# A second level of seven products inside four of the block products of q, k and v

## The chip, the cores and the metric

The kernel runs on one core of a Trainium2 chip. The metric is device time in microseconds (us) of one execution. TensorE (PE) multiplies, VectorE (DVE), ScalarE (ACT) and GpSimd (POOL) do elementwise work, SyncE (SP) issues most of the DMA transfers. A matmul reads a stationary operand of 128 x 128, loaded by its own instruction (PEld), and streams the columns of the other operand past it. Results go to PSUM, in tiles that are handed from engine to engine by semaphores.

## The reference

Two graph layers over 4096 nodes with 512 features, each followed by a residual sum and a layer norm. The first is a masked additive attention with 4 heads. The second, cut to what matters here, is

```
q = einsum('nd,hdk->hnk', x, Wqs)      # x: 4096 x 512, 8 heads of 64
k = einsum('nd,hdk->hnk', x, Wks)
v = einsum('nd,hdk->hnk', x, Wvs)
scores = einsum('hqk,hmk->hqm', q, k) / 8 + 0.01 * eye - 1e16 * (1 - adj)
x = layernorm(x + einsum('hqm,hmk,hko->qo', softmax(scores), v, Wo))
```

So q, k and v are each a product of a 4096 x 512 matrix and a 512 x 512 matrix, all in fp32.

## The kernel before

The program has three stages on its time line: layer 0 (to about 1126 us), the q, k, v stage (to about 1420 us), and the attention of layer 1 (to the end). All engines work through queues in the written order.

**The q, k, v stage.** The loop `for pair in range(NG // 2)` goes over four pairs of 512 rows, and calls `gemm` three times in each: k, q, v. In a gemm the 1024 rows by 512 features of a pair and the 512 x 512 weights are each cut into 2 x 2 blocks (`features(pair, c, n)`, `block(w, m, c)`), and the block product is done with seven products instead of eight. The products have numbers, and `order = (1, 5, 2, 6, 7, 3, 4)` is the order in which TensorE does them. Products 5, 6, 7 and 3 read sums of weight blocks (`combine_weights`, tables `of_weights`, `wk_s`, `wq_s`, `wv_s`), and products 5, 6, 7 and 4 read sums of feature blocks (`combine_features`, `x_s`). The sums of the weights are made once, in the gemms of pair 0; those of the features are made for each pair, in the v gemm of the pair before, on VectorE (L1176).

A product is 2 x 2 x 2 chunk products of 128 features by 128 outputs by 256 rows. For k and q (L1208) it is four matmuls of 512 columns; for v (L1201), in which the features are the stationary operand, eight of 256 columns. An fp32 matmul is two passes on TensorE, each with its own weight load, and the profile counts passes. Products 2, 3 and 4 accumulate onto the PSUM tile of products 1, 5 and 7.

The results leave PSUM thus: ScalarE copies product 1 to `u2`, product 5 to `p5`, and product 1 + 2 to the first output block (L1215); VectorE adds product 6 onto `u2` and `u2` onto the others (L1236); GpSimd adds `p5` to the fourth block (L1230). `store` sends blocks to DRAM from SP's queue. PSUM holds three tiles of two banks (`s_ps`) and two tiles of one bank (`x_ps`).

What a gemm does beside its products is in a table `beside`: after product i the functions of `beside[i]` are issued. Here lie the loads of the next rows (`bring`), their transposes on VectorE (`turn`, L975), the sums of weights and features, and, in the last pair, the loads for the attention (`load_adjT`, `load_q`, `load_kv`). `Later` holds steps that are issued some products later; in the first two gemms these are the layer norms that end layer 0 (`normal_factors`, four small GpSimd instructions each, L514 to L519).

In SBUF the tag `adjT1` has 11 places, for blocks of the mask in the attention. In the q, k, v stage `spare()` lends them to the sums.

**Attention.** In the last v gemm, before product 4, TensorE does the scores of the first three units (`score`, L1138), so that the attention's pipeline is full when the gemm ends. In the attention TensorE alternates between scores (L1138) and products with v (L1424).

Of the kernel before, what the change touches and what calls it, by code (L numbers as in the profile page):

```python
# [429 lines left out]
def tile_gat_then_masked_attention(  # L430
# [666 lines left out]
    with wait_by_tile("l1", 1) as l1, wait_by_tile("l1a", 2) as lp, \  # L1097
# [46 lines left out]
        with wait_by_tile("l1s", 2) as sp:  # L1144
# [9 lines left out]
            def spare():  # L1154
# [4 lines left out]
            wq_s = {5: wq_s[0][:, 0], 6: wq_s[0][:, 1], 3: wq_s[1][:, 0], 7: block(wq, 1, 0)}  # L1159
            wv_s = {i: sp.tile([P, 2, D // 2], F32, name=f"wv_s{i}", bufs=1) for i in (5, 6, 3)}  # L1160
            wv_s[7] = block(wv, 1, 0)
            x_s = {i: spare().rearrange("p a b r -> p (a b r)").rearrange(
                "p (c r) -> p c r", c=2) for i in of_features}

            def features(pair, c, n):
                return xTs[2 * pair + n][:, 2 * c:2 * c + 2, :]

# [5 lines left out]
            def combine_features(engine, pair, i):  # L1173
                a, c, op = of_features[i]
                a, c = (x_s[k] if isinstance(k, int) else features(pair, *k) for k in (a, c))
                engine.tensor_tensor(x_s[i], a, c, op=op)  # L1176
# [4 lines left out]
            def gemm(w, sums, kind, pair, beside):  # L1181
# [5 lines left out]
                u2, p5 = (sp.tile([P, 2 * G], F32, name=n, bufs=2) for n in ("u2", "p5"))  # L1187
# [4 lines left out]
                def product(i, t, more=False):  # L1192
                    a = block(w, *plain_weights[i]) if i in plain_weights else sums[i]
                    x = features(pair, *plain_features[i]) if i in plain_features else x_s[i]
                    for n in range(2):
                        half = t[0][:, n * G:(n + 1) * G] if len(t) == 1 else t[n]
                        if kind == "v":
                            half = half.rearrange("p (t d) -> p t d", t=2)
                            for r in range(2):
                                for c in range(2):  # L1200
                                    nc.tensor.matmul(  # L1201
                                        half[:, r, :],
                                        x[:, c, (2 * n + r) * P:(2 * n + r + 1) * P], a[:, c, :],
                                        start=not more and r == 0 and c == 0, stop=c == 1,
                                        skip_group_check=True)
                        else:
                            for c in range(2):
                                nc.tensor.matmul(half, a[:, c, n * P:(n + 1) * P], x[:, c, :],  # L1208
                                                 start=not more and c == 0, stop=c == 1,
                                                 skip_group_check=True)  # L1210

# [20 lines left out]
                def add(dst, t):  # L1232
                    n = 2 * G // len(t)
                    for k, src in enumerate(t):
                        part = slice(k * n, (k + 1) * n)
                        nc.vector.tensor_tensor(dst[:, part], src, u2[:, part], op=ALU.add)  # L1236

                t = {}
                for i in order:
                    if i == (7 if last else 1 if kind == "k" and pair == 0 else 0):  # L1240
                        t[i] = [xp.tile([P, GT, P], F32, name="x_ps").rearrange(
                            "p t r -> p (t r)") for _ in range(2)]
                    elif i in (1, 5, 6, 7):
                        t[i] = new()
                    else:
                        t[i] = t[{2: 1, 3: 5, 4: 7}[i]]
                    if i == 4 and last:
                        for n in range(3):
                            first[n] = score(0, 0, n)
                            nc.scalar.activation(first[n], first[n], AF.Exp, scale=float(KD) ** -0.5)  # L1250
# [8 lines left out]
                    elif i == 6:  # L1259
                        add(u2, t[i])  # L1260
                    elif i == 7:
                        add(out["22"], t[i])
                        pool(out["22"], out["22"], p5, ALU.add)
                        later.at(1, lambda: store("22"))
                    elif i == 3:
                        add(out["12"], t[i])
                        store("12")
                    elif last:
                        copy(out["21"], t[i])
                        pool(out["21"], out["21"], u2, ALU.add)  # L1270
                        store("21", nc.gpsimd)
                    else:
                        add(out["21"], t[i])
                        store("21")
                    for fn in beside.get(i, []):
                        fn()
                    later.step()

            for pair in range(NG // 2):
# [10 lines left out]
                beside = {}  # L1290
                if pair == 0:
                    combine_features(nc.vector, 0, 5)
                    for n, i in ((1, 6), (5, 7), (2, 3)):
                        beside.setdefault(n, []).append(
                            lambda i=i: combine_weights(nc.vector, wk, wk_s, i))
                    for n, i in ((1, 6), (5, 7), (2, 4)):
                        beside.setdefault(n, []).append(
                            lambda i=i: combine_features(nc.vector, 0, i))
                    for i, n in ((5, 7), (6, 7), (7, 3), (3, 4)):
                        beside.setdefault(n, []).append(  # L1300
                            lambda i=i: combine_weights(nc.gpsimd, wq, wq_s, i))
                if more:
                    for k, n in ((5, 0), (7, 1)):
                        beside.setdefault(k, []).append(lambda n=n: bring(n))
                if pair == 0:
                    beside.setdefault(4, []).append(lambda: load_all(wv, wvs))
                gemm(wk, wk_s, "k", pair, beside)
                beside = {}
                if pair == 0:
                    for i, n in ((5, 5), (6, 2), (7, 6), (3, 7)):  # L1310
                        beside.setdefault(n, []).append(
                            lambda i=i: combine_weights(nc.gpsimd, wv, wv_s, i))
                if more:
                    for k, fn, n in ((1, turn, 0), (5, turn, 1), (5, bring, 2), (6, bring, 3),
                                     (4, turn, 2)):
                        beside.setdefault(k, []).append(lambda fn=fn, n=n: fn(n))
                else:
                    for c in range(3):
                        load_adjT(0, c)
                    load_q(0, 0)  # L1320
                gemm(wq, wq_s, "q", pair, beside)
                beside = {}
                if more:
                    beside[1] = [lambda: turn(3)]
                    for i, n in ((5, 5), (6, 6), (7, 7), (4, 4)):
                        beside.setdefault(n, []).append(
                            lambda i=i: combine_features(nc.vector, pair + 1, i))
                else:
                    beside[5] = [lambda: load_kv(0, 0, 0)]
                    beside[2] = [lambda: [load_adjT(0, c) for c in range(3, NCJ - 2)],  # L1330
                                 lambda: [finish_md(0, t) for t in range(GT)]]
                    beside[7] = [lambda: load_kv(0, 0, 1),
                                 lambda: [load_adjT(0, c) for c in range(NCJ - 2, NCJ)]]
                gemm(wv, wv_s, "v", pair, beside)
# [282 lines left out]
```

## Time and profile before

| | |
|---|---|
| median of three runs | 3333.77 us (3333.41 to 3334.64) |
| profiled execution, its own time | 3333.58 us |
| its span, first to last instruction | 3331.7 us |
| granted TensorE clock | 0.998 |
| PE busy | 3310.5 us, 99% |
| DVE, ACT, POOL busy | 72%, 59%, 63% |
| k or q gemm | 24.0 us |
| v gemm | 24.17 us |

The page gives the busy time of each engine, the chain of work that ended last, and groups of instructions by line. In a row of the timeline, the first number is the start in us from the span's start, the second the duration of the instruction or of the group (`x8` is eight instructions), then engine, line, operation, output and inputs; in brackets stands the idle time before it and what ended it. Names lose their numbers, and a lent tile bears the name of its place: `adjT` in this stage is a sum of weights or features, and `p` is often `p5`. A row of the table of stretches has the stretch, its length, busy time and instructions of PE, PEld, DVE, ACT and POOL, the granted clock, the busy share of the DMA engines and GB/s.

### The profile page before, as it was taken

Reading aid. Unit: us, or ns where it says so; the run is one execution under the profiler, and the core shown is the slowest. Engines: PE = TensorE matmul, PEld = TensorE weight load, DVE = VectorE, ACT = ScalarE, POOL = GpSimd, SP = SyncE. Lnnn points to the kernel's source line nnn. Section 1 sums busy time; section 2 is a strip of 40 time slices with the busy share of each in tenths; the row PEclk is TensorE's granted clock in tenths of the full one; section 3 lists DMA queues with packets and bytes.
Section 4 is the critical chain, followed back from the end, with each engine's and each line's share of the span. In section 5 each row is a group of like instructions: output and inputs, shape, how many; then the busy total and the mean of one; then the engine's idle time right before and its main releaser. Section 6 shows DMA issues by size and latency. Waiting matters only on the chain.

```text
span 3331.7 us, 66521 instructions
## 1 busy us (share of the span) xinstructions
PE 3310.5 (99%) x26968; PEld 1938.6 (58%) x26968; DVE 2403.4 (72%) x3005; ACT 1955.9 (59%) x2419; POOL 2106.7 (63%) x1535
## 2 busy tenths in 40 slices
PE   9999999999999999999999999999999999999998
PEld 8899999999999756633333333333333333333333
DVE  6789899898999633266767666666766766667666
ACT  1367968878766311156656556566565656656654
POOL 5630040040030310189999999999999999999996
PEclk9999999999999999999999999999999999999999
DMA  8989786686532443489898988989888799887984
GB/s 180 229 203 184 220 185 169 152 181 146 137 93 58 115 147 111 160 198 212 191 214 224 225 204 189 211 191 253 206 191 210 188 208 251 193 211 185 211 198 112
DMA packets 398989, 612.01 MB, mean 184 GB/s; under 512 B 167632, under 2 KB 248528, under 8 KB 398672
## 3 DMA queue, kind: packets, MB, share of 16 engines
q0 software_dynamic: 97520, 258.77, 42.6%
q1 hardware_dynamic: 299280, 345.88, 33.3%
q8 instruction: 214, 3.51, 0.4%
q10 hardware_dynamic: 1872, 3.02, 0.4%
q14 instruction: 103, 0.84, 0.1%
HBM read 315.87 MB, written 109.25 MB: 128 GB/s over the span
## 4 chain that ended last, share of the span: by engine, by line
PE 95%; POOL 2%; DMA 1%; DVE 1%; issue 1%; ACT 0%; SPq 0%; POOLq 0%; DVEq 0%
PE o_ps L1087 27%; PE o_ps L1424 26%; PE s_ps L1138 25%; PE s_ps L1208 6%; PE o_ps L846 4%; PE s_ps L1488 3%; PE s_ps L1201 3%; DMA p<-p 1%; PE s_ps L1443 1%; POOL q_sum L1399 0%; DMA y_sb<-in_x_dram 0%; DVE p L1556 0%; POOL s L699 0%; PE x_ps L1201 0%; PE x_ps L1208 0%
## 5 line engine op out<-in xcount | busy, mean ns | idle before, releaser
L1399 POOL TENSOR_TENSOR q_sum<-q_sum,p 128x1024 f32<-128x1024 f32 x538 | 1373.0, 2552 | 63.8 <-DMA p<-p 38.1
L1379 DVE TENSOR_TENSOR p<-s_ps,adjT 128x1024 f32<-128x1024 f32 x896 | 1044.0, 1216 | 464.8 <-ACT s_ps L1376 437.3
L1376 ACT ACTIVATE s_ps<-s_ps 128x1024 f32<-128x1024 f32 x1021 | 967.3, 1006 | 594.4 <-PE s_ps L1138 591.6
L1138 PE MATMUL s_ps<-q_sb,k_sb 64*64 64x512 f32 x8192 | 943.0, 589 | 0.7 <-DVE p L1379 0.7
L1424 PE MATMUL o_ps<-p,v_sb 64*64 64x512 f32 x8192 | 943.6, 590 | 0.0
L1087 PE MATMUL o_ps<-sup_t,p 128*128 128x129 f32 x8192 | 915.7, 275 | 1.2 <-DVE p L640 1.2
L1087 PEld LDWEIGHTS o_ps<-sup_t,p 128*128 128x128 f32 x8192 | 915.3, 192 | 1.7 <-DVE p L640 1.4
L640 DVE SCALAR_TENSOR_TENSOR p<-fr_t,dj,az 128x1024 f32<-128x1024 f32 x512 | 650.4, 1284 | 67.1 <-PE o_ps L1087 38.9
L1138 PEld LDWEIGHTS s_ps<-q_sb,k_sb 64*64 64x64 f32 x8192 | 312.7, 133 | 567.0 <-issue 455.4
L1424 PEld LDWEIGHTS o_ps<-p,v_sb 64*64 64x64 f32 x8192 | 310.3, 133 | 570.6 <-issue 561.2
L624 ACT ACTIVATE z<-fr_t,f 128x1024 fp8e4<-128x1024 f32 x512 | 557.2, 1143 | 101.6 <-DVE az L635 101.5
L1409 POOL DMA_DIRECT2D p<-p x412 | 437.7, 1300 | 9.3 <-PE o_ps L1424 8.4
L1063 POOL DMA_DIRECT2D agg<-base_d x32 | 29.0, 1215 | 386.8 <-DMA sup_t<-sup_d 204.7
L585 POOL COPY seen<-token 128x1 f32<-128x1 f32 x24 | 11.4, 476 | 356.4 <-DVE token L583 356.4
L1379 DVE TENSOR_TENSOR p<-s_ps,md 128x1024 f32<-128x1024 f32 x128 | 150.6, 1217 | 69.4 <-ACT s_ps L1376 64.4
L635 DVE TENSOR_TENSOR az<-adjT,z 128x512 int32<-128x512 int32 x256 | 175.3, 685 | 1.9 <-ACT z L624 0.7
L1230 POOL TENSOR_TENSOR k_sb<-k_sb,p 128x1024 f32<-128x1024 f32 x12 | 30.7, 2560 | 192.1 <-DVE k_sb L1236 187.8
L600 ACT ACTIVATE adjT<-stage 128x1024 fp8e4<-128x1024 bf16 x128 | 130.8, 1050 | 17.8 <-DMA stage<-adj_d 17.8
L1215 ACT ACTIVATE u<-s_ps 128x1024 f32<-128x1024 f32 x11 | 11.3, 1024 | 173.4 <-PE s_ps L1208 110.1
L1488 PE MATMUL s_ps<-wo_sb,on 128*128 128x512 f32 x240 | 110.8, 604 | 0.0
L1458 ACT ACTIVATE r<-r_h 32x256 f32<-32x256 f32 x248 | 102.3, 412 | 2.9
L1236 DVE TENSOR_TENSOR u<-s_ps,u 128x1024 f32<-128x1024 f32 x12 | 14.7, 1225 | 106.2 <-PE s_ps L1208 76.3
(194 smaller groups left out, 2094.4 us busy)
## 6 DMA issues: line engine op xcount, KB each, us to landing
p<-p POOLq DMA_DIRECT2D x412, 512.0 KB, 9.1
k_sb<-k_d SPq DMA_DIRECT2D x128, 512.0 KB
v_sb<-v_d SPq DMA_DIRECT2D x128, 512.0 KB
adj_d<-in_adj_dram POOLq DMA_DIRECT2D x32, 1024.0 KB, 11.3
sup_t<-sup_d SPq DMA_DIRECT2D x120, 258.0 KB
fr_t<-fr_d SPq DMA_DIRECT2D x16, 1024.0 KB
adjT_d<-adjT SPq DMA_DIRECT2D x32, 512.0 KB
adjT<-adjT_d SPq DMA_DIRECT2D x32, 512.0 KB
```

What stands on the lines that cost most here:

```text
L624: nc.scalar.activation(z[:, k, :], fr_t[w, h][:, 0, :], AF.Sign, bias=fs[j // GT][:, 0, (j + k) % GT, h:h + 1], saturate=False)
L635: nc.vector.tensor_tensor(az.bitcast(I32), adjT[w, j // CJ][:, j % CJ:j % CJ + 2, :].bitcast(I32), z.bitcast(I32), op=ALU.bitwise_and)
L640: nc.vector.scalar_tensor_tensor(p, fr[:, 1, :], dj[j // GT][:, j % GT, h:h + 1], az_t[w, h, j // 2][:, j % 2, :], op0=ALU.max, op1=ALU.mult)
L1087: nc.tensor.matmul(o[t // BK][:, t % BK, :], p[:, t * P:(t + 1) * P], s, start=(j == 0 and t % BK == 0), stop=(j == NT - 1), skip_group_ch ...
L1138: nc.tensor.matmul(s[c:c + MS, e, :], k[r, a + c:a + c + MS], qt[g, m][r, :], start=True, stop=True)
L1208: nc.tensor.matmul(half, a[:, c, n * P:(n + 1) * P], x[:, c, :], start=not more and c == 0, stop=c == 1, skip_group_check=True)
L1376: nc.scalar.activation(s, s, AF.Exp, scale=float(KD) ** -0.5)
L1379: nc.vector.tensor_tensor(p, s, keep[:, None, :].to_broadcast([P, HP, G]), op=ALU.mult)
L1399: nc.gpsimd.tensor_tensor(q, q, p, op=ALU.add)
L1409: later.at(2, lambda: nc.gpsimd.dma_start(a, b, accum_op=ALU.add))
L1424: nc.tensor.matmul(o[c, n, :], v[r, j % CH, c], p[r, e, :], start=(j == 0), stop=(j == NT - 1))
L1488: nc.tensor.matmul(s, on_t[g][:, m, t * P:(t + 1) * P], wo_sb[:, m, :], start=(m == 0), stop=(m == NP1 - 1))
```

## The change

In ten of the twelve gemms (k and q of pairs 1 to 3, v of all pairs) the products 1, 5, 6 and 7 are split once more: their 2 x 2 x 2 chunk products become seven, of 256 columns for k and q and of two times 128 columns for v. `deep = (1, 5, 6, 7)` names them. Products 2, 3 and 4 stay whole, but go to PSUM tiles of their own and are added up on VectorE. The order becomes a plan of pairs (product, phase): `begin` does chunk products 1, 5, 6, 7, and `end` does 2, 3, 4.

New sums of chunks are needed: `combine_weights2` (tiles `w2_s`) on VectorE for k and q and on GpSimd for v, once; `combine_features2` (tiles `x2_s`) on GpSimd for each pair. The feature sum 7 is now written over the block that it comes from. All 11 places of `adjT1` are lent, one of them to `abs_`, into which ScalarE copies half of a tile. In the last pair only one block of the mask is loaded ahead of the v gemm instead of three, three blocks follow product 5 and four follow product 7, and the second k and v load follows product 4. `turn(2)` moves from product 4 of q to product 7 in pairs 1 and 2.

```diff
+            deep = (1, 5, 6, 7)
...
+            for i in (1, 5, 6, 7, 4):
+                if i in deep:
+                    x2_s[i] = flat().rearrange("p (i r) -> p i r", i=4)
+                if i in (5, 6, 4):
+                    x_s[i] = flat().rearrange("p (c r) -> p c r", c=2)
+            abs_ = flat().rearrange("p (i r) -> p i r", i=2)
+            w2_s = {n: sp.tile([P, len(deep), 3, P], F32, name=f"w2_s{n}", bufs=1)
+                    for n in ("k", "q", "v")}
...
+            def combine_weights2(engine, kind, w, sums, i):
+                for k in (5, 6, 7, 3):
+                    a, c, op = of_weights[k]
+                    a, c = (of_w2(kind, w, sums, i, n) if isinstance(n, int) else
+                            of_w(w, sums, i)[:, n[1], n[0] * P:(n[0] + 1) * P] for n in (a, c))
+                    engine.tensor_tensor(of_w2(kind, w, sums, i, k), a, c, op=op)
+
+            def combine_features2(engine, pair, i):
+                for k in (5, 6, 7, 4):
...
+                    engine.tensor_tensor(of_x2(pair, i, k), a, c, op=op)
...
+                def small(i, k, dst, start):
+
+                    a, x = of_w2(kind, w, sums, i, k), of_x2(pair, i, k)
+                    if kind == "v":
+                        for r in range(2):
+                            nc.tensor.matmul(dst[:, r * P:(r + 1) * P], x[:, r * P:(r + 1) * P], a,
+                                             start=start and r == 0, stop=True,
+                                             skip_group_check=True)
+                    else:
+                        nc.tensor.matmul(dst, a, x, start=start, stop=True, skip_group_check=True)
...
+                def begin(i, dst, base):
+
+                    t = new()[0]
+                    q = [t[:, k * HG:(k + 1) * HG] for k in range(4)]
+                    for k, at, start in ((1, 0, True), (5, 1, False), (6, 3, True), (7, 2, False)):
+                        small(i, k, q[at], start)
+                    ab = abs_[:, (1, 5, 6, 7).index(i) % 2]
+                    nc.scalar.activation(ab, t[:, 0:G], AF.Copy)
+                    v2, p5s = ab[:, 0:HG], ab[:, HG:G]
+                    if base is None:
+                        sum_(v2, q[3], v2)
+                        sum_(part(dst, 1, 1), shape(q[2]), shape(v2))
+                    else:
+                        sum_(q[3], q[3], v2)
+                        if kind == "v":
...
+                            sum_(both, b, shape(q[3])[:, None].to_broadcast([P, 2, 2, P]))
+                            sum_(part(dst, 0, 1), shape(q[3]), part(base, 0, 1))
+                        else:
...
+                            sum_(both, b, q[3][:, None].to_broadcast([P, 3, HG]))
+                        sum_(part(dst, 1, 1), shape(q[2]), part(dst, 1, 1))
+                    pool(part(dst, 1, 1), part(dst, 1, 1), shape(p5s), ALU.add)
+                    held[i] = t, q, v2, dst, base
+
+                def end(i):
+                    t, q, v2, dst, base = held.pop(i)
+                    for k, at in ((2, 0), (3, 1), (4, 2)):
+                        small(i, k, q[at], False)
...
+                    if i == 6:
+                        pool(out["12"], u2, p5, ALU.add)
+                    elif i == 7:
+                        pool(out["22"], u2, p5, ALU.add)
...
+                plan = [(i, 2) for i in order]
+                if deep:
+                    plan = [(1, 0), (5, 0), (1, 1), (5, 1), (2, 2), (6, 0), (3, 2), (6, 1), (7, 0)]
+                    plan += [(4, 3), (7, 1), (4, 2)] if last else [(4, 2), (7, 1)]
...
+                    for n, i in ((2, 1), (6, 5), (7, 6), (3, 7)):
+                        beside_at(n, combine_weights2, nc.vector, "k", wk, wk_s, i)
+                    for n, i in ((1, 1), (5, 5), (2, 6), (6, 7)):
+                        beside_at(n, combine_features2, nc.gpsimd, 0, i)
+                    for n, i in ((3, 5), (3, 1), (4, 6), (4, 7)):
+                        beside_at(n, combine_weights2, nc.gpsimd, "v", wv, wv_s, i)
```

## The prediction

> **What bounds it now.** I read the page's engine shares and its chain first: they say which engine sets the end.
>
> ```profile
> PE 3310.5 (99%) x26968; PEld 1938.6 (58%) x26968; DVE 2403.4 (72%) x3005; ACT 1955.9 (59%) x2419; POOL 2106.7 (63%) x1535
> ...
> PE 95%; POOL 2%; DMA 1%; DVE 1%; issue 1%; ACT 0%; SPq 0%; POOLq 0%; DVEq 0%
> ```
>
> TensorE is busy throughout and carries the chain. The change lies in the q, k, v stage, so I asked for the chain in order of time there (start, length, instructions).
>
> ```profile
> 1099.93 26.13 PE o_ps L1087 x234
> 1126.06 3.43 PE x_ps L1208 x8
> ...
> 1136.36 37.77 PE s_ps L1208 x88
> 1174.13 24.17 PE s_ps L1201 x112
> 1198.30 48.07 PE s_ps L1208 x112
> ```
>
> The stage is 12 gemms of seven block products, 3.43 us each (24.17 / 7 = 3.45 for v), with no gap: it starts at 1126.06 and a saved TensorE microsecond is a saved microsecond, as the attention behind it is TensorE too. The table of stretches (busy PE, PEld, DVE, ACT, POOL) shows the slack of the others: two stretches inside the stage.
>
> ```profile
> 1198.00:1222.00 24.00, 24.00 (x58) 10.76 (x57) 6.03 (x5) 3.07 (x3) 2.34 (x1) 1.00 0.56 160
> ...
> 1246.00:1270.00 24.00, 24.00 (x112) 20.95 (x111) 11.02 (x15) 3.07 (x3) 3.21 (x1) 1.00 0.20 67
> ```
>
> There VectorE works 6 to 11 of 24 us. In pair 0 GpSimd is not idle: its timeline in the q gemm of pair 0 shows what any added sum must queue with.
>
> ```profile
> 1162.19 1.26 POOL L1171 TENSOR_TENSOR wv_s<-wv 128x512 f32<-128x512 f32 x1 [7.08 <-DMA wv<-in_L_gnn_Wvs_dram]
> ...
> 1164.96 1.26 POOL L1171 TENSOR_TENSOR wv_s<-wv_s,wv 128x512 f32<-128x512 f32 x1
> ...
> 1168.95 2.34 POOL L1230 TENSOR_TENSOR k_sb<-k_sb,p 128x1024 f32<-128x1024 f32 x1
> 1171.25 1.27 POOL L1171 TENSOR_TENSOR wv_s<-wv,wv_s 128x512 f32<-128x512 f32 x1
> ```
>
> It can't begin on wv before 1162.19, when the load lands, and is done at 1172.5, barely before the v gemm at 1174.13.
>
> **What is removed.** Ten gemms (k and q of pairs 1 to 3, v of all) do products 1, 5, 6, 7 as 7 instead of 8 chunk products. One chunk product of k or q is a matmul of 256 columns in two passes; 112 passes of 256 columns took 24.17 us, 0.216 each, so 0.43 a chunk: 24 products save 24 x 0.43 = 10.3. In v a chunk is two matmuls of 128 columns, four passes. The nearest row is the 129-column pass of L1087: 26.13 / 234 = 0.112. Seven chunks are 28 x 0.112 = 3.13 instead of 3.43: 16 x 0.30 = 4.8. Removed: **15.1 us**. (PEld lasts 192 ns in L1087 too, so were loads not overlapped a product would take 28 x 0.19 = 5.3; the 0.112 spacing excludes most of that.)
>
> [...]
>
> **What is added, and what waits.** Durations: ACT 512 columns 0.60 (L1215). VectorE 512 and 1024 columns 0.69 and 1.23; on that line 256 are 0.42, 128 are 0.29. GpSimd 1.27 and 2.34 give 0.73 and 0.46. I take this line for GpSimd's 20 new sums ahead of (a), as 128x1 (0.19, L518) lies on it too; the bounds are 0.23 (128x1, L519) and 1.27 (512 columns) each, which would make the wait of (a) 2.5 or 23 instead of 10.4. Handovers: PE to ACT or VectorE 0.26, ACT to VectorE 0.04, VectorE to itself 0.08, VectorE to POOL 0.14, VectorE to PE 0.25 with the restart.
>
> *(a) First v gemm.* GpSimd must make v's chunk sums in the q gemm of pair 0, behind chunk sums of the features. From 1162.19 until those that v's first products read (i = 5, then 1): four wv sums 5.0, the add 2.3, two layer-norm groups of 1.4 (1163.54 to 1164.96 is one) 2.8, 12 feature sums x 0.73 = 8.8, 8 weight sums x 0.46 = 3.7: 22.6, so 1184.8. TensorE asks at 1174.13 + 0.45 = 1174.6; with 0.2 of handover it waits 10.4. In these microseconds VectorE also makes 8 to 12 wk chunk sums of 0.29 with both inputs in SBUF. Do such sums hold GpSimd up? The trace:
>
> ```profile
> 1192.58 1.22 DVE L1176 TENSOR_TENSOR adjT<-xT 128x1024 f32<-128x1024 f32 x1
> ...
> 1192.81 3.19 POOL L1230 TENSOR_TENSOR k_sb<-k_sb,p 128x1024 f32<-128x1024 f32 x1 [12.39 <-DVE k_sb L1236]
> ...
> 16.27 1.65 POOL L804 TENSOR_TENSOR p<-xT,p 128x512 f32<-128x512 f32 x1 [1.83 <-DVE p L799]
> ...
> 16.71 1.75 DVE L763 TENSOR_TENSOR w_sb<-w_sb 128x512 f32<-128x512 f32 x1
> ```
>
> Beside a VectorE sum of two SBUF operands the GpSimd add took 3.19 instead of 2.34; begun first, GpSimd made VectorE take 1.75 instead of 0.68. Adds with one PSUM operand (L1236) don't show it: 2.34. So +0 to 3.5, I take 1.6: **12.0**.
>
> [...]
>
> *(b) k and q gemms, six.* After the first four chunks, ACT copies, VectorE adds twice (the second needs the first), and only then may TensorE write on in that tile: 0.26 + 0.60 + 0.04 + 0.42 + 0.08 + 0.42 + 0.25 = 2.07. Product 5's four chunks cover 1.71: wait 0.36. Product 5's own rest is covered by 1.28 + 0.36 of product 1's rest: wait 0.43. Product 7's rest stands behind VectorE's add into u2, which must wait until GpSimd has read u2 for out12: from the end of product 6, 0.26 + 0.33 (0.42 less the 0.09 by which VectorE's instructions overlap) + 0.69 + 0.14 + 2.34 + 0.14 + 0.96 + 0.08 + 0.42 + 0.25 = 5.61, covered by 1.71 + 3.43 = 5.14: wait 0.47. Each saves 1.71 and waits 1.27: 6 x 1.27 = **7.6**.
>
> *(c) Starts of v gemms.* In pairs 0 and 3 0.28 and 0.45 by the same chain (cover 1.79): 1.5. In pairs 1 and 2 four transposes of turn(2), moved to product 7 of q, stand in VectorE's queue ahead of these adds (4 x 0.34): 1.36 twice. **4.2**.
>
> *(d) Ends of v gemms of pairs 0 to 2 and the k behind.* VectorE holds feature sums of 1.23 and GpSimd 16 chunk sums x 0.73 = 11.7 of 25 us; alone 0.6 a pair (1.7), each meeting paid in series 2.3 (6.9). I take **5.0**.
>
> *(e) Entry to the attention.* The second early score needs the tile of product 3, freed by a VectorE add that now stands behind product 7's first adds, which wait for GpSimd: 2.2, and 0.8 as exp and mask catch up: **3.0**. The loads: adjT 4 to 7 (2 MB) and two stores now precede k and v of chunk 1 on SP, in front of scores of units 8 on. 3 MB at the 237 GB/s of the last v stretch before is 12.7 us, needed within about 12: 0 to 4, I take 0, as adjT now leaves some 5 us before the end.
>
> q's chunk sums on VectorE in the k gemm of pair 1 (16 x 0.29 = 4.6 of some 23 us), in which it has 8 to idle, and ACT's copies (half as wide) cost nothing under that cover; without it, up to 4.6.
>
> **Sum.** -15.1 + 12.0 + 7.6 + 4.2 + 5.0 + 3.0 = +16.7. The profiled execution took 3333.58 (span 3331.7 and 1.9 around it; median of the runs 3333.77), so 3350.3: I say **3350**.
>
> **Rivals.** *Faster, by one mechanism:* GpSimd is in time. It decides at 1174.6: 22.6 us of queue would have to fit in 12.4. Its old work takes 10.1, leaving 2.3 for 20 sums, 0.12 each, under even the 0.23 of a 128x1 instruction; and (b) to (e) must fall as well. With all waits gone: 3333.6 - 15.1 = 3318.5; with (a) alone gone, 3338. Chance of a time under 3327: 0.07. *No change:* waits are finer than I take them: TensorE's second chunks wait for ACT's copy alone. Then (b) is 6 x 0.47 = 2.8, (c) 2.7, and with lone-engine values for (a), (d) and (e) the sum is -15.1 + 10.4 + 2.8 + 2.7 + 1.7 + 3.0 = +5.5, 3339. For it: products of before show waits of whole tiles only, so nothing tells. 0.14. [...] 0.2. *Loads decide in v:* 0.19 a pass, 16 x 1.9 = 30 more than before instead of 4.8 less: 3385; L1087 speaks against it. 0.03. My own case: 0.56.
>
> **Range and chances.** From the no-change case to just past the slower one: 3336 to 3362. About 0.2% (6.7 us) is what a measurement of this kernel can tell from no change. Faster 0.07, same 0.14, slower 0.79.
>
> **What would show it.** Right: the first v gemm holds one TensorE wait of 10 to 14 us put down to POOL's chunk sums (w2_s); k and q gemms take about 23.5 instead of 24.0 us; v gemms of pairs 1 and 2 about 25, longer than before; VectorE is the releaser of waits of 0.3 to 1.4. Wrong: no TensorE wait over 5 us at 1174; v gemms near 23; or passes of 128 columns spaced at 0.19; or a TensorE wait on a k_sb load in the first attention units.

## The result, and the profile after

The changed kernel takes **3356.36 us** (median of four runs, 3351.68 to 3359.32) against 3334.11 us: a ratio of **1.0066, 95% interval 1.0048 to 1.0083**. It is slower, by 22 us; predicted were 3350, with a range from 3336 to 3362. The profiled execution took 3353.77 us, of which the span is 3352.0. It is 20.3 us longer than the span before, and this is what is explained here.

The page's shares of busy time and of the chain, after:

```profile
PE 3305.7 (99%) x27304; PEld 1973.8 (59%) x27304; DVE 2493.4 (74%) x3210; ACT 1959.1 (58%) x2449; POOL 2218.4 (66%) x1665
...
PE 51%; POOL 3%; DMA 2%; DVE 1%; issue 1%; ACT 0%; POOLq 0%; SPq 0%; DVEq 0%; ACTq 0%
```

TensorE is busy 4.8 us less (3310.5 before) and the end comes 20.3 us later: about 25 us more in which it stands. The chain's shares add up to 58%, because it can be followed back only to 1381 us. From there to the attention it runs through GpSimd, VectorE and DMA too, where before it was TensorE alone. The waits of TensorE in the stage (who waited for whom, us in total, times, longest) say for what:

```profile
PE s_ps L1269 <- POOL w_sv L1208: 9.5, 1, 9.5
PE s_ps L1269 <- DVE u L1312: 4.4, 5, 1.0
PE s_ps L1138 <- DMA k_sb<-k_d: 2.7, 1, 2.7
PE s_ps L1273 <- DVE u L1312: 1.6, 4, 0.5
PE s_ps L1138 <- DVE v_sb L1299: 1.5, 1, 1.5
PE s_ps L1273 <- DVE p L1312: 1.1, 5, 0.3
...
```

L1269 and L1273 are the chunk products of v and of k and q, L1138 the scores; before, this stage had no such row. Times from the first matmul of one gemm to that of the next, from the traces of four kernels (two of them experiments below), put the waits in their places:

| us | before | after | k, q split alone | the same, reordered |
|---|---|---|---|---|
| k and q, pair 0 (whole in all) | 48.07 | 48.07 | 48.07 | 48.07 |
| v, pair 0 | 24.17 | 36.53 | 24.17 | 24.17 |
| k and q, pair 1 | 48.07 | 47.35 | 46.67 | 45.23 |
| v, pair 1 | 24.17 | 25.15 | 24.17 | 24.17 |
| k and q, pair 2 | 48.07 | 47.33 | 46.71 | 44.77 |
| v, pair 2 | 24.17 | 25.15 | 24.17 | 24.17 |
| k and q, pair 3 | 48.07 | 47.33 | 46.72 | 44.77 |
| v of pair 3, to the attention's first product | 29.83 | 32.14 | 29.83 | 29.83 |
| from there to product 200 | 42.06 | 44.92 | 42.06 | 42.06 |
| products 200 to 8000 | 1790.6 | 1792.8 | 1791.7 | 1792.4 |

Of the 20.3 us, 12.4 are the first v gemm, 2.0 the v gemms of pairs 1 and 2, 5.2 the last one and the attention's entry, 2.2 the rest of the attention; k and q give back 2.2. The remaining 0.7 lies ahead of the stage and after product 8000.

**The first v gemm.** TensorE's timeline (start, length, instructions; in brackets the idle time and its end) and GpSimd's, with the first chunk sum that had to wait and the one that TensorE waited for:

```profile
1174.29 0.61 PE L1269 MATMUL s_ps<-wv,xT 128*128 128x128 f32 x4
1184.42 2.08 PE L1269 MATMUL s_ps<-w_sv,adjT 128*128 128x128 f32 x8 [9.52 <-POOL w_sv L1208]
...
1189.41 0.61 PE L1269 MATMUL s_ps<-wv_s,adjT 128*128 128x128 f32 x4
1189.86 0.61 PE L1269 MATMUL s_ps<-wv,xT 128*128 128x128 f32 x4
```

```profile
1162.63 1.27 POOL L1220 TENSOR_TENSOR wv_s<-wv 128x512 f32<-128x512 f32 x1 [4.21 <-DMA wv<-in_L_gnn_Wvs_dram]
1163.86 0.72 POOL L1215 TENSOR_TENSOR adjT<-adjT 128x256 f32<-128x256 f32 x1
...
1182.14 0.45 POOL L1208 TENSOR_TENSOR w_sv<-wv_s 128x128 f32<-128x128 f32 x1
...
1183.91 0.46 POOL L1208 TENSOR_TENSOR w_sv<-wv 128x128 f32<-128x128 f32 x1
```

From 1162.63 to 1184.37 GpSimd is never idle, with durations near those of the prediction (0.72 to 0.86 us for 256 columns and 0.46 for 128, against 0.73 and 0.46). One thing is new. The four passes from 1189.41 and those from 1189.86 are 0.45 apart, 0.112 a pass; the 24 passes between 1184.42 and 1189.41 took 4.99 us, 0.208 each. The table of stretches (length, PE, PEld, DVE, ACT, POOL, then the granted clock, DMA share, GB/s) says why:

```profile
1176.00:1178.00 2.00, 0.00 (x0) 0.00 (x0) 1.98 (x5) 0.00 (x0) 1.83 (x4) 1.00 0.00 0
1178.00:1180.00 2.00, 0.00 (x0) 0.00 (x0) 0.61 (x2) 0.00 (x0) 1.83 (x4) 0.71 0.00 0
1180.00:1182.00 2.00, 0.00 (x0) 0.00 (x0) 0.00 (x0) 0.00 (x0) 2.00 (x2) 0.50 0.08 32
...
1186.00:1188.00 2.00, 2.00 (x12) 2.00 (x10) 0.00 (x0) 0.60 (x1) 1.67 (x6) 0.50 0.33 125
1188.00:1190.00 2.00, 2.00 (x15) 2.00 (x15) 0.85 (x2) 0.00 (x0) 1.92 (x6) 0.73 0.00 0
```

While TensorE stood, its clock was halved, from 1.00 to 0.50, and it stayed halved until 1189.1 (0.73 in the last stretch), 4.7 us into the work. The 24 passes cost 24 x (0.208 - 0.112) = 2.3 us on top of the wait.

**The attention's entry.** The chain of work in order of time, from the end of the last v gemm's products on (start, length, what):

```profile
1421.57 2.36 POOL v_sb L1293
...
1425.30 1.14 DVE v_sb L1299
...
1430.40 2.34 POOL k_sb L1293
...
1433.18 4.27 DMA v_d<-k_sb
...
1437.47 4.81 DMA k_sb<-k_d
1442.28 0.14 issue
1442.41 1.09 PE s_ps L1138 x8
```

GpSimd's sum for out22 ends at 1432.74, its store lands at 1437.45, and only then is the load of the next block of k issued, into the place that the store has freed. TensorE stood 2.66 us for it.

### The profile page after: what moved, and what is told of

Same layout as the page of the kernel before. It is cut to its first block, busy times and chain, and to the rows that moved or that the text cites. A ratio compares the mean times of both kernels' runs of the same rounds, so it can differ in the third digit from the quotient of the medians.

```text
span 3352.0 us, 67714 instructions
## 1 busy us (share of the span) xinstructions
PE 3305.7 (99%) x27304; PEld 1973.8 (59%) x27304; DVE 2493.4 (74%) x3210; ACT 1959.1 (58%) x2449; POOL 2218.4 (66%) x1665
## 3 DMA queue, kind: packets, MB, share of 16 engines
q10 hardware_dynamic: 1872, 3.02, 0.4%
## 4 chain that ended last, share of the span: by engine, by line
PE 51%; POOL 3%; DMA 2%; DVE 1%; issue 1%; ACT 0%; POOLq 0%; SPq 0%; DVEq 0%; ACTq 0%
PE o_ps L1608 23%; PE s_ps L1138 23%; PE s_ps L1672 3%; DMA p<-p 2%; POOL q_sum L1583 2%; POOL p L1593 1%; PE s_ps L1627 1%; PE s_ps L1260 0%; DVE p L1563 0%; PE s_ps L1269 0%; POOL q_sum L1579 0%; DVE p L1740 0%; PE s_ps L1273 0%; PE s_ps L1253 0%; PE o_ps L1672 0%
## 5 line engine op out<-in xcount | busy, mean ns | idle before, releaser
L1138 PE MATMUL s_ps<-q_sb,k_sb 64*64 64x512 f32 x8192 | 944.8, 589 | 7.3 <-DVE p L1563 3.0
L1138 PEld LDWEIGHTS s_ps<-q_sb,k_sb 64*64 64x64 f32 x8192 | 315.2, 133 | 571.5 <-issue 450.2
L1593 POOL DMA_DIRECT2D p<-p x412 | 439.0, 1305 | 12.3 <-PE o_ps L1608 12.3
L1323 ACT ACTIVATE adjT<-s_ps 128x512 f32<-128x512 f32 x40 | 23.9, 598 | 198.7 <-PE s_ps L1273 102.3
L1049 ACT ACTIVATE agg<-o_ps,rinv 128x128 f32<-128x128 f32 x128 | 41.9, 368 | 69.1 <-DVE den L1042 47.9
L1672 PEld LDWEIGHTS s_ps<-wo_sb,on 128*128 128x128 f32 x240 | 43.3, 189 | 55.9 <-issue 55.4
```

The costliest lines, as they stand in the source:

```text
L1138: nc.tensor.matmul(s[c:c + MS, e, :], k[r, a + c:a + c + MS], qt[g, m][r, :], start=True, stop=True)
L1593: later.at(2, lambda: nc.gpsimd.dma_start(a, b, accum_op=ALU.add))
L1672: nc.tensor.matmul(s, on_t[g][:, m, t * P:(t + 1) * P], wo_sb[:, m, :], start=(m == 0), stop=(m == NP1 - 1))
```

## The experiments

The theory before them: GpSimd's chunk sums and the half clock that follows make the first v gemm; waits for VectorE, all short, make the others; the place that a late store frees makes the entry. The rivals: a backlog that is only handed on, VectorE and GpSimd shutting each other out, a half clock that comes anyway, DMA engines too full.

**1. The first v gemm whole.** Pair 0's feature chunk sums are not made; v's weight chunk sums move into that gemm.

```diff
...
-                gemm(wv, wv_s, "v", pair, beside, deep)
+                gemm(wv, wv_s, "v", pair, beside, deep if pair else ())
```

> The first v gemm is whole again, so pair 0's feature chunk sums are not made, and v's weight chunk sums are made on GpSimd during that gemm instead of ahead of it. All else is as in the changed kernel. My theory (the wait for GpSimd's chunk sums is the largest term, and the half clock from 1178.8 to 1189.1 us follows from it): the v gemm of pair 0 takes 24.2 us again instead of 36.5, no stretch at half clock is left in mid-kernel, and 12.4 us come off the median of 3356.4: 3344 (3341 to 3347). Rival 1 (GpSimd's backlog is only handed on: its sums come late for the k gemm of pair 1 or the v gemm of pair 1): the 24.2 us are there, but a wait of 4 us or more for GpSimd shows up later, 3348 or more. Rival 2 (the half clock comes whatever the wait): 3346, with a stretch of about 10 us at 0.5 somewhere between 1130 and 1440 us.

Measured: 3340.55 us (3337.12 to 3344.62), ratio 1.0024 (1.0014 to 1.0033). The first v gemm takes 24.17 us, the clock is 1.00 through it, and the gemms after it are as in the changed kernel (47.31, 25.16, 47.33, 25.14, 47.32). The stage is 12.4 us shorter, as expected; the median fell 15.8 us, more than the stages account for, to just under the expected range (see experiment 5). Rival 2 falls, and rival 1 in its size: TensorE has no later wait that is put down to GpSimd. A small rest is handed on: GpSimd makes chunk sums until 1207.5 us, well into the next k gemm, where TensorE has a wait of 0.41 us for VectorE, which itself had waited 0.62 us for GpSimd. Pair 1's k and q take 47.31 us, 0.64 more than in experiment 3, which has no such sums. What is left of the loss, 6.4 us on the median, is in the v gemms behind and at the entry.

**2. The last v gemm whole**, with the order of early scores, loads and stores of the kernel before. (This gemm then reads chunks of wv that chunk sums have been written over, so that its v is not what the reference asks for; its instructions are those of a whole gemm.)

```diff
...
-                gemm(wv, wv_s, "v", pair, beside, deep)
+                gemm(wv, wv_s, "v", pair, beside, deep if more else ())
```

> Only the last v gemm is whole again, with the kernel before's order of the early scores, of the loads and of the stores around it; all other gemms are split as in the changed kernel. My theory (the attention's entry lost 2.3 us to the last gemm's late sums and 2.9 us to the load of k_sb that waits for the place which the late out22 store frees): 5.2 us come off, 3351 (3349 to 3353), from the last v gemm's first matmul to the first products 29.8 us, and no wait of L1138's scores for a load. Rival 1 (the loads are late because the whole stage's stores crowd the queues, not because of that place): the wait of 2.7 us for k_sb<-k_d stays, 3354. Rival 2 (the 2.3 us that the attention loses after product 4000 also comes from how it is entered): 3349 or less, and product 8000 stands where product 200 stands.

Measured: 3347.38 us (3346.29 to 3349.55), ratio 1.0041 (1.0027 to 1.0055). From the last gemm's start to the first product 29.83 us, to product 200 another 42.06 us, both as in the kernel before; no wait of L1138 at the entry. So the 5.2 us are that gemm's, and rival 1 falls. The time lies under the expected range, where rival 2 had it; but rival 2 falls by the trace: products 200 to 8000 took 1793.5 us here, more than in the changed kernel. The profiled execution is 5.3 us shorter than that of the changed kernel; what the median fell beyond that may lie in the changed kernel's own spread (experiment 5).

**3. k and q of pairs 1 to 3 split alone.**

```diff
...
-                gemm(wv, wv_s, "v", pair, beside, deep)
+                gemm(wv, wv_s, "v", pair, beside)
```

(v's and pair 0's chunk sums go; the last pair's loads and scores stand as in the kernel before.)

> Only the k and q gemms of pairs 1 to 3 are split; the four v gemms are whole, v's and pair 0's chunk sums are not made, and the attention is entered as in the kernel before. My theory (a split k or q gemm saves 1.7 us of passes and loses 1.3 us in three waits for VectorE): each pair's k and q take 47.35 us instead of 48.07, v gemms 24.17, nothing is lost at the entry, 3334.1 - 3 x 0.72 = 3331.9 (3331 to 3333), a little faster than the kernel before. Rival 1 (sums and adds on VectorE and GpSimd shut each other out once v's own sums are off GpSimd too; my prediction's serial case): 48.1 us per pair, no gain, 3334. Rival 2 (the lost 2 us in the attention belong to the split gemms' leavings): 3334 to 3336 with the 0.72 us gained per pair.

Measured: 3330.09 us (3327.45 to 3332.66), ratio 0.9987 (0.9977 to 0.9996): faster. That is under the expected range, and both rivals, which have no gain, fall. A pair takes 46.7 us, not the 47.35 of the changed kernel. So a split v gemm costs twice: 0.98 us itself and 0.64 us in the k and q behind it. Split v in pairs 1 and 2 is a loss of 1.6 us each. (How the 0.64 comes about is not shown. Pair 1 has it in experiment 1 too, behind a whole v gemm in which GpSimd makes v's chunk sums.)

**4. A shorter wait:** 8 of the feature chunk sums of pair 0 on VectorE.

```diff
-                    for n, i in ((1, 1), (5, 5), (2, 6), (6, 7)):
+                    for n, i in ((1, 1), (5, 5),):
                         beside_at(n, combine_features2, nc.gpsimd, 0, i)
+                    for n, i in ((2, 6), (6, 7),):
+                        beside_at(n, combine_features2, nc.vector, 0, i)
```

> As the changed kernel, but pair 0's feature chunk sums for products 6 and 7 (8 sums of 256 columns) are made on VectorE instead of GpSimd, which takes 8 x 0.75 us = 6.0 us from the queue that the first v gemm waits for. My theory: the wait falls from 9.5 us to about 3.5 to 4.1 us, VectorE hides its 8 x 0.42 us, and 6 us come off: 3350. If the half clock needs a long wait, it goes too, 2.4 us more: 3348. Rival 1 (VectorE and GpSimd shut each other out, so that moved sums save nothing): wait of 7 us or more, 3354. Rival 2 (any wait of some us brings the half clock): 3350 with a stretch of about 10 us at 0.5 beginning near the wait.

Measured: 3347.05 us (3344.59 to 3351.49), ratio 1.0040 (1.0028 to 1.0053). The wait for GpSimd fell from 9.5 to 4.3 us and the gemm from 36.53 to 31.53; VectorE's extra sums cost 0.64 us in pair 0's k and q. The clock fell all the same, to 0.50 from 1177.9 to 1184.8 us. Rival 1 falls, rival 2 stands. The next run shortens the wait further.

**5. The changed kernel again,** unaltered.

> The changed kernel itself, unaltered, beside the others of this call. Its first four times spread from 3351.7 to 3359.3 us, and kernels with one of its waits taken out came out 2 to 4 us lower than the stages of their traces account for. If that is the chip and the hour, it gives 3351 to 3355 here; if the changed kernel itself spreads, again a median of 3355 to 3357 with 5 us and more between its runs. By stages it should show the wait of 9.5 to 10.1 us and one stretch of about 10 us at half clock again.

Measured: 3353.88 us (3351.75 to 3355.14), 2.5 us under its first median, as the first of the two cases had it, and a ratio of 1.0062 (1.0047 to 1.0078). Against this median experiment 1 is 13.3 us lower, near the 12.4 of its stages. The first v gemm takes 37.04 us with a wait of 9.8. In this execution the entry's wait of 2.8 us for k_sb brought a second stretch at half clock (1443.6 to 1447.0 us), and product 200 came 46.47 us after the first instead of 44.92. The same code has it in one execution and not in the other: a part, at least, of the spread of the changed kernel's times.

**6. A wait shorter still:** 12 of the 16 sums on VectorE.

> As the changed kernel, but pair 0's feature chunk sums for products 5, 6 and 7 (12 sums of 256 columns) are made on VectorE instead of GpSimd, 12 x 0.75 us = 9.0 us off the queue that the first v gemm waits for. My theory (TensorE's clock halves only if TensorE stands for some 3 us or more: with a wait of 4.3 us in the experiment before this one the clock fell 2.6 us into it, and half clock then cost 2.4 us): a wait of 1.0 to 1.6 us is left, the clock stays at 1.00 throughout, the first v gemm takes 26.0 to 26.7 us against 31.5 there, and 5 us come off: 3342 (3340 to 3344). Rival 1 (the half clock comes with any wait, or with the small passes): 28.5 us and a stretch at 0.50, 3344.5. Rival 2 (VectorE takes so much longer with four more sums that TensorE waits for it instead): more than 0.64 us on pair 0's k and q, or waits for DVE at the start of the v gemm that add up to over 2 us, 3345 or more.

Measured: 3343.49 us (3342.83 to 3347.70). The time is within what was expected, the reasons are not. The wait left is 2.5 us, not 1.0 to 1.6; the extra sums cost 1.3 us in pair 0's k and q (49.39), as rival 2 has it, if not to its 3345 us; and the clock fell although the wait was short. TensorE's timeline and the stretches:

```profile
1177.98 1.33 PE L1269 MATMUL s_ps<-w_sv,adjT 128*128 128x128 f32 x8 [2.52 <-POOL w_sv L1208]
```

```profile
1178.00:1179.00 1.00, 1.00 (x8) 0.99 (x9) 1.00 (x2) 0.00 (x0) 0.99 (x3) 1.00 0.51 191
1179.00:1180.00 1.00, 1.00 (x8) 1.00 (x7) 1.00 (x4) 0.00 (x0) 0.83 (x3) 0.51 0.21 82
1180.00:1182.00 2.00, 2.00 (x11) 2.00 (x11) 1.10 (x3) 0.60 (x1) 1.75 (x6) 0.50 0.58 221
1182.00:1183.00 1.00, 1.00 (x9) 1.00 (x9) 0.00 (x0) 0.00 (x0) 1.00 (x3) 0.79 0.00 0
```

TensorE was at work again at 1177.98, and the clock halved at 1179.0, a microsecond later, for 3.4 us. My theory of a wait of 3 us or more falls; rival 1 is right in that some waits under 3 us bring it, wrong in that any does (after waits of 1.5 us and less no trace here shows it; the last section has those between).

**7. The sum for out22 on VectorE** in the last v gemm.

```diff
-                        pool(out["22"], u2, p5, ALU.add)
+                        (sum_ if last else lambda *a: pool(*a, ALU.add))(out["22"], u2, p5)
```

> As the changed kernel, but in the last v gemm the sum for out22 (u2 + p5, 1024 columns) is made on VectorE (about 1.25 us) instead of GpSimd (2.35 us). My theory (the attention's second load of k waits for the place that out22's store frees, and that store waits for this sum): the store is issued about 1.1 us earlier, and TensorE's wait for k_sb<-k_d falls from 2.7 us to between 0.5 and 1.6 us; the 1.2 us in VectorE's queue delay the adds behind it, so that the first products come up to 1.2 us later, and of the time up to product 200 between -1.5 and +0.5 us comes off. Rival (the load is late because 13 loads and 8 stores crowd the DMA engines): the wait stays at 2.5 us or more.

Measured (one run): 3354.54 us. The first product came 0.64 us later (32.78), and the wait for k_sb<-k_d was 2.4 us: the theory's 0.5 to 1.6 is missed, the rival's 2.5 nearly met. The wait alone tells little: in the profiles of kernels with the changed kernel's entry it was 2.7 and 2.8 (the changed kernel twice), 1.3, 1.5 and 3.0 us (experiments 4, 6 and 9), and 2.8 us in experiment 1, there put down to VectorE's `p`. SP's queue in the changed kernel and then in this one (the second kernel's last v gemm began 1.5 us later):

```profile
1427.46 2.15 SPq L1105 DMA_DIRECT2D adjT<-adjT_d  x4
1432.76 0.92 SPq L1284 DMA_DIRECT2D v_d<-k_sb  x2
1437.47 0.33 SPq L1123 DMA_DIRECT2D k_sb<-k_d  x1
...
1444.38 0.32 SPq L1123 DMA_DIRECT2D k_sb<-k_d  x1
```

```profile
1433.06 0.98 SPq L1284 DMA_DIRECT2D v_d<-k_sb  x2
1439.12 0.33 SPq L1123 DMA_DIRECT2D k_sb<-k_d  x1
```

From the store's issue to the load's it took 4.71 us in the changed kernel (4.15 to 5.43 in the other kernels with its entry), and 6.06 us here. Counted from the start of the gemm, the store was issued 1.2 us sooner and the load no sooner: the store stood behind something, and ahead of it on the queue are four loads of 512 KB. (The 0.2 to 0.3 us by which the next expectation has the load earlier are counted from the first product, which came 0.64 us later.)

**8. These four loads behind the store and the load of k.**

```diff
-                        beside_at(7, load_adjT, 0, c)
+                        beside_at(4, load_adjT, 0, c)
```

> As the changed kernel, but the last four adjT loads (512 KB each) are issued behind the store of out22 and the second loads of k and v instead of ahead of them. It tells apart what delays the load of k that the attention's entry waits 2.4 to 2.8 us for. With the sum for out22 made 1.2 us earlier on VectorE the load came only 0.2 to 0.3 us earlier, so that the sum's lateness is not what decides. My theory now (the store's 4.3 to 5.6 us to landing are the DMA engines' queue, which the adjT loads issued from 1427.5 us on keep at a share of 0.95 to 1.05): without them ahead the store lands within 2 to 2.5 us, the load of k follows about 2 us earlier and is itself served at once, the wait for k_sb<-k_d falls to 0.5 us or less, the time up to product 200 from 44.9 to 42.2 to 42.8 us, and 2 to 3 us come off: 3351. Rival (the store's and the load's own durations, one after the other): 2 us of the wait or more stay, 3353.5.

Measured: 3357.46 us (3354.05 to 3359.51), ratio 1.0071 (1.0054 to 1.0088); no gain, where 3351 was expected. The cause is shown, the cure fails:

```profile
1433.23 0.91 SPq L1284 DMA_DIRECT2D v_d<-k_sb  x2
1436.50 0.33 SPq L1123 DMA_DIRECT2D k_sb<-k_d  x1
...
1437.37 2.12 SPq L1105 DMA_DIRECT2D adjT<-adjT_d  x4
...
1447.42 0.32 SPq L1123 DMA_DIRECT2D k_sb<-k_d  x1
```

With the loads out of its way, the store's place is free after 3.27 us instead of 4.71 (the theory had 2 to 2.5), the wait of 2.66 us is gone (product 24 comes 5.36 us after the first, 5.15 in the kernel before). But the 2 MB now stand ahead of the third block of k, whose load is issued at 1447.42 instead of 1444.38 and which TensorE awaits for longer, by its timeline:

```profile
1459.09 3.55 PE L1138 MATMUL s_ps<-q_sb,k_sb 64*64 64x512 f32 x16 [4.04 <-DMA k_sb<-k_d]
```

with a stretch at half clock behind it. So the entry's 2.7 us are 2 MB of mask, which by the code can't be loaded before product 7, as all 11 places are lent; in the kernel before they were loaded ahead of the last products, at a DMA share of 1.01 to 1.06 from 1408 to 1418 us.

**9. The third turn of transposes back behind product 4.**

> As the changed kernel, but the third turn of transposes (4 of about 0.4 us on VectorE) stands behind product 4 of q in all pairs again, as in the kernel before, not behind product 7. My theory (these transposes delay VectorE's sums at the start of the v gemms of pairs 1 and 2, a wait of 1.0 us there): the wait for u at their start falls by 0.4 to 0.7 us, and 25.15 us become 24.4 to 24.8 each. Rival (the waits at the start are the sums' own chain, copy and add after the first four small products): 25.0 to 25.2 us as they are.

Measured (one run): 3351.73 us; the v gemms of pairs 1 and 2 take 24.87 us instead of 25.15. Between theory and rival: the first wait, 1.05 us, is gone, but others, of which the profile shows one of 0.15 us, take most of its place. With the transposes out of the way the sums' own chain is next.

**10. k and q split alone, the sum for out12 on VectorE.**

```diff
-                        pool(out["12"], u2, p5, ALU.add)
+                        sum_(out["12"], u2, p5)
```

> As the kernel with k and q of pairs 1 to 3 split alone (46.7 us for a pair's k and q), with one step of the reordering: the sum for out12 (u2 + p5, 1024 columns) is made on VectorE instead of GpSimd. My theory (each of these gemms has one wait of about 0.45 us, at the second part of product 7, because VectorE's add for out12 stands in its queue until GpSimd's 2.35 us sum is done): 2 x 0.4 to 0.5 us come off a pair, 45.7 to 45.9 us, so that the step from there to the 44.8 us of the reordered kernel is the early product 2; 3330.1 - 2.7 = 3327.4 (3326 to 3329). Rival (VectorE is full, and 1.25 us more in its queue only move the wait): 46.5 us or more, 3330.

Measured: 3329.68 us (3327.60 to 3331.64), ratio 0.9986 (0.9976 to 0.9996). A pair takes 46.3 us, 0.4 less, half of the gain expected; by the median (3330.09 without it) it can't be told from nothing. The wait at product 7, 0.2 us in each gemm of experiment 3, is gone; it had been 0.2, not the 0.47 of the prediction. The waits that the profile still shows, 0.27 and 0.52 us, are at the ends of products 1 and 5.

**11. k and q split alone, reordered.** Besides that sum: product 2 fills the gap ahead of the ends of products 1 and 5, q's chunk sums move to the first v gemm, the transposes behind products 2, 3 and 7.

```diff
-                    plan = [(1, 0), (5, 0), (1, 1), (5, 1), (2, 2), (6, 0), (3, 2), (6, 1), (7, 0)]
+                    plan = [(1, 0), (5, 0), (2, 3), (1, 1), (2, 2), (5, 1), (6, 0), (3, 2), (6, 1), (7, 0)]
```

(Phase 3 and phase 2 of product 2 are its two halves; the add into out11 follows the end of product 5.)

> k and q of pairs 1 to 3 split, v whole (as in the experiment that split k and q alone), and then every wait that was left taken on: product 2 is issued in two halves between the second product's first part and the ends of products 1 and 5; the sum for out12 is made on VectorE instead of GpSimd; q's chunk sums are made during the first v gemm; the transposes of the next pair stand behind products 2, 3 and 7 of q. My theory (passes saved are worth 1.7 us a gemm, and only waits of 0.36, 0.43 and 0.48 us eat them): k and q of a pair take 44.6 to 45.2 us against 48.07 in the kernel before and 46.7 with k and q split alone, three times 3.0 to 3.4 us: 3324 (3322 to 3327), faster than the kernel before by 0.3%. Rival 1 (VectorE becomes the bound: the out12 sum adds 1.25 us to it in every gemm): waits for DVE move to the ends of products 6 and 7, 46 us or more per pair, 3328 to 3331. Rival 2 (passes of 128 rows by 256 columns wait for weights when nothing else does): 46 us with no waits shown.

Measured: **3324.78 us** (3322.14 to 3326.02), ratio **0.9973 (0.9964 to 0.9983)**: faster than both kernels. A pair takes 45.23, 44.77 and 44.77 us; the only wait that the profile shows in the stage is one of 0.22 us in pair 1. The chain in order of time is TensorE without a gap again, chunk products (L1273) and whole ones (L1260):

```profile
1206.47 3.02 PE s_ps L1273 x14
1209.49 3.43 PE s_ps L1260 x8
1212.92 3.02 PE s_ps L1273 x14
```

VectorE works 17.7 of the 24 us from 1222 to 1246 (7.5 before): it is not the bound. The stretch in the kernel before and in this one:

```profile
1222.00:1246.00 24.00, 24.00 (x57) 10.64 (x56) 7.53 (x12) 3.07 (x3) 2.35 (x1) 1.00 0.41 131
```

```profile
1222.00:1246.00 24.00, 24.00 (x89) 16.61 (x88) 17.73 (x31) 3.16 (x6) 6.83 (x6) 1.00 0.58 154
```

Rivals 1 and 2 fall. Seven chunk products take 3.02 us instead of 3.43. Of the 1.9 us that a pair gained on experiment 3, the sum for out12 alone had brought 0.4; product 2, q's chunk sums and the transposes were not tried apart.

## Why the prediction was right, and where it was not

The verdict, the place and the largest mechanism were right. Four of the sizes were not, and they cancelled in part. The first v gemm's wait came out at 9.5 us, just under the 10 to 14 that were to show it right; and one sign of being wrong came true, a wait of TensorE on a k_sb load at the attention's entry.

- **Removed (15.1).** Right for k and q: 48.07 - 44.77 = 3.30 us for eight chunk products without waits, 0.41 each, against 0.43. For v the spacing of 0.112 is shown (four passes in 0.45 us), so that loads don't decide; a v gemm without waits was not made.
- **(a) The first v gemm, 12.0.** The wait of 10.4 measured 9.5: TensorE needed five of the eight weight sums, not all. The surcharge of 1.6 for meetings of VectorE and GpSimd is the term that was too large. GpSimd's sums of 256 columns took 0.72 to 0.86 in that stretch, some 0.5 us in all over the shortest. It was VectorE that paid more: its sums, the shortest of which took 0.28, beside a GpSimd sum of 1172.75 to 1174.06 us and the next:

```profile
1172.98 1.24 DVE L1208 TENSOR_TENSOR w_sk<-w_sk,wk 128x128 f32<-128x128 f32 x1
1174.14 0.81 DVE L1208 TENSOR_TENSOR wk<-wk 128x128 f32<-128x128 f32 x1
1174.87 0.28 DVE L1208 TENSOR_TENSOR w_sk<-wk,w_sk 128x128 f32<-128x128 f32 x1
```

  The size is what the prediction missed: the longest of GpSimd's sums of 256 columns beside them took 0.86 where 0.73 was reckoned, 0.13 more, and VectorE had time. In experiments 4 and 6 the sums moved to VectorE did cost, 0.64 and 1.3 us.
- **The half clock, not priced: 2.3.** The trace of before had shown it, at 12 to 20 us, behind a wait of TensorE of 3.05 us (a granted clock of 0.88 and 0.69 in stretches of 4 us); I read a mean of 0.998 and looked no further.

```profile
12.00:16.00 4.00, 1.89 (x7) 1.60 (x8) 3.65 (x7) 1.88 (x2) 1.27 (x1) 0.88 1.06 311
16.00:20.00 4.00, 4.00 (x14) 3.29 (x13) 3.12 (x4) 1.05 (x2) 3.45 (x6) 0.69 1.12 209
```

- **(b) k and q, 7.6.** Waits of 1.27 a gemm measured 3.30 - 1.37 = 1.93 for the two of a pair without split v (48.07 - 46.70 = 1.37 gained), 0.97 a gemm. The step that failed is product 7's: 0.2 instead of 0.47; the two at products 1 and 5 came to 0.76, against 0.79. In the changed kernel itself a pair lost 3.30 - 0.73 = 2.57, 1.28 a gemm. That this meets the 1.27 is luck: 0.64 of it goes with the split v gemms, which the prediction has under (d).
- **(c) and (d), starts and ends of v, 9.2.** For pairs 1 and 2 they were 1.36 + 1.67 - 1.2 saved = 1.83 each; measured 0.98 + 0.64 = 1.62. About right, with a start of 1.05 instead of 1.36.
- **(e) The entry, 3.0, and the loads at 0.** The scores waited 1.45 for v_sb and 0.72 for p, 2.2 in all. The step that failed is the loads, of which the bounds were 0 to 4: they cost 2.7. I had counted bytes against a deadline; what decided is a chain, sum, store, place, load, behind 2 MB in the same queue.
- **The rest of the attention, not priced:** 2.2 us in the profiled execution. The edits don't explain it: products 200 to 8000 took 1790.6 before, and between 1790.7 (the changed kernel again) and 1793.5 (its last v gemm whole) in the eleven profiles of the experiments. It goes with the execution, and in the profile it stands as TensorE's waits for VectorE's `p`: 2.3 us in four of them, 0.7 us in two before. Why they vary stays open.

By product 200 the terms that were priced came to 17.6 - 0.3 (ahead of the stage) - 2.3 (half clock) - 2.7 (the load) = 12.3 us instead of 16.7. The half clock, which was not priced, and the load, which was put at 0, added 5.0: that the total came near is in part luck. The upper end of the range, 3362, rests on a slower case in which every meeting of VectorE and GpSimd is paid in full: 10.4 + 3.5 = 13.9 us for the first wait, 1.36 + 2.3 - 1.2 = 2.46 for a split v gemm of pairs 1 and 2. No run shows these sizes: the first wait was 9.5 us, and a split v gemm cost 1.62. The median lies in the range all the same, so that the terms refute this case and the time does not. Of the rivals, no change, with waits for ScalarE's copy alone, is refuted by the waits for VectorE's adds; that weight loads decide in v, by the spacing; GpSimd in time, by its timeline.

## What to carry to other kernels

A split that saves TensorE passes pays only if what releases its next pass is done by then: list the releasers of each product, and put a product that waits for nothing in each gap. Here that order, three smaller moves beside it, and leaving v alone turned +22 us into -9; one sum moved between engines, alone, brought 0.4 us a pair. A tile place that is lent for sums is also a load that comes late: follow it to the next stage. And a wait of TensorE can cost more than itself: behind the one of 2.5 us in experiment 6 the clock stood at 0.50 for 3.4 us.

## What the runs showed of the hardware

TensorE's granted clock was halved after some waits and not after others. In the q, k, v stage and behind the attention's entry it stood at 0.50 for 3.4 us after waits of 2.5 us (experiment 6), 2.8 us (experiment 5) and 4.0 us (experiment 8), for 6.8 us after the one of 4.3 us (experiment 4), and for 10.2 us after those of 9.5 to 10.1 us for GpSimd's chunk sums. In experiment 6 it fell a microsecond after the wait; where it fell during the wait, the half clock ended 2.7 to 5.1 us after work had begun again.

The length of the wait alone does not decide. At the attention's entry waits of 2.4 us (experiment 7), 2.66 us (the first profile of the changed kernel), 2.8 us (experiment 1) and 3.0 us (experiment 9) left the clock at 1.00, and the one of 2.8 us in the second profile of the changed kernel halved it. The stretches of the first profile and then of the second (length, busy time of PE, PEld, DVE, ACT and POOL, granted clock, DMA share, GB/s):

```profile
1440.00:1444.00 4.00, 1.59 (x16) 0.78 (x20) 2.35 (x2) 1.32 (x2) 1.62 (x2) 1.00 1.04 321
1444.00:1448.00 4.00, 4.00 (x40) 1.63 (x36) 1.23 (x1) 1.57 (x3) 0.85 (x1) 1.00 0.98 258
```

```profile
1440.00:1444.00 4.00, 1.42 (x16) 0.26 (x8) 2.42 (x3) 1.93 (x2) 3.29 (x3) 0.95 0.99 269
1444.00:1448.00 4.00, 3.73 (x24) 1.44 (x28) 0.75 (x2) 1.01 (x1) 0.00 (x0) 0.62 1.07 293
```

What decides is not shown.
